# A four-layer gated cross-attention network on one core: plans made in stages, weights, mask, keys and a context moved to other places, biases added by TensorE

## The chip, the cores and the metric

The kernel runs on one core of one Trainium2 chip. A run's time is the device time in microseconds; runs are compared by their medians. Three runs of the kernel before took 1714.19, 1714.95 and 1720.62 us. One further execution was taken by the hardware profiler; its rows are called "the profile" or "the trace" here. Five engines work side by side, each through its own queue of instructions: TensorE (PE for its matmuls, PEld for its weight loads), VectorE (DVE), ScalarE (ACT), GpSimd (POOL) and SyncE (SP), which here only issues DMAs.

## The reference

The input x has 16 sequences of 128 tokens with 256 numbers each, and there is a context of the same shape. Four layers follow each other, each a cross attention and then a feed-forward part; both are added to x after a multiplication by the tanh of a gate:

```
for i in 0..3:
    x = x + tanh(g_xattn[i]) * attention_i(layernorm(x), ctx)
    x = x + tanh(g_ffn[i])   * ffn_i(layernorm(x))
```

Attention 0 has 16 heads and no biases; 1 has biases and takes its softmax over the queries; 2 takes its queries from x and adds a key mask times -1e30, with biases; 3 has 8 heads of 64 and attends over the normed context together with the normed x. Feed-forward 0 routes every token to 2 of 8 experts (GELU, hidden 1024); 1 is a dense layer with a LoRA mixture and a bias; 2 routes to 2 of 8 experts with a clipped SwiGLU and adds a shared expert with a bias; 3 routes to 2 of 8 experts (SiLU, hidden 256). All numbers are float32.

## The kernel before

**Blocks.** Tokens lie on the 128 partitions; x stays in SBUF as 16 tiles of 128x256. Four sequences make a block, so there are four blocks.

**Attention loop.** `attend` (line 1181) writes the order of the instructions of PE, ACT and DVE out by hand: within it these three engines keep program order. A step per sequence emits scores, values of the sequence before and output of the one before that. Between these pieces `tick()` (1193) advances side jobs, which are Python generators: preparing the next block (`prepare`: queries, keys, normed contexts), and the work behind a finished block (`behind`: routing or LoRA). A job yields a number, the count of ticks until its next turn, cut to `most` (5 in layer 0, 99 in layers 1 and 2, 2 in layer 3) and to 1 once the last scores are emitted; from then on a filler, such as expert slots, also takes a turn per tick. Layers 1 and 2 share one call of `attend`. A block's first step waits in the program until its preparing jobs are emitted.

**Work outside that loop**, and DMA issue on SP and POOL inside it, is ordered by a list scheduler with a cost model: it may put an instruction ahead of others that the program creates earlier, where it thinks that an engine is free.

**Routing.** `Moe.front` (360) norms a block, computes router logits, picks two experts for each token with DVE operations of 0.15 to 0.25 us, ranks the tokens with two small matmuls (389) and scatters every token's row twice to DRAM (`xg`) with eight indirect DMAs on POOL (443). `Moe.plan` (497 to 589) then computes, in some 25 DVE operations, which expert each slot of 128 rows has and where its rows begin (`plan_i`, 570); SP reads these numbers into registers. Layer 0 has an early plan after block 1 and a last one after block 3, layer 2 has one, layer 3 three (after blocks 1, 2 and 3). A slot of an early plan needs only the scatters made until then.

**Slots.** `Moe.slots` (591) runs 39 slots of 128 rows per routed layer: SP loads the rows (653) and, where the expert changes, the weights (1256); PE transposes the rows (686), multiplies twice (1303, 1472 or 1520, then 723); POOL scatters the result to `yd` (732). Three lanes of weights take turns. In layer 0 nine early slots run inside the attention loop as its filler, and the others after it.

**What lies where before the change.** The eight DMAs of the attention weights of layers 1 and 2 (815, called at 2043) are created between the early slots and the others of layer 0; `mask_by_keys` (1900), which makes two columns per sequence out of layer 2's mask, right after them. The shared expert's weights (1388) are loaded ahead of the loop of layers 1 and 2. Each layer's keys (1021) are projected one block ahead; only layer 1 makes two blocks of keys at its start. `first_context` (1737) norms layer 3's context of block 0 at the end of layer 2's slots, `context` (1743) the others in the loop. Output biases of attentions 1 and 2, LoRA and the shared expert are scaled with the gate by DVE (281) and added to x by POOL (`add_bias`, 284), 64 operations of 128x256.

**Range check.** The fast path leaves out the softmax maximum. `Watch.see` (972) clamps each reciprocal to a range and adds up what the clamp changed, in three POOL operations; at the end, a count decides whether the whole network is computed again in the general way. It isn't here.

Of the kernel before, what the change touches and what calls it, by code (L numbers as in the profile page):

```python
# [37 lines left out]
TINY, HUGE = 1e-30, 1e30  # L38
# [51 lines left out]
def kernel(ctx: ExitStack, tc: tile.TileContext, a: dict, out: bass.AP):  # L90
# [51 lines left out]
    for e in range(2):  # L142
        nc.gpsimd.memset(ones2[:, e, e, :], 1.0)
# [3 lines left out]
    tg = const.tile([P, 8], F32, tag="tg", name="tg")  # L147
# [11 lines left out]
    nc.gpsimd.memset(nothing, 0.0)  # L159
    region = const.tile([P, NE], F32, tag="region", name="region")  # L160
# [12 lines left out]
    token_i = const.tile([P, B], I32, tag="token_i", name="token_i")  # L173
# [9 lines left out]
    def tgx(i):  # L183
        return tg[:, i:i + 1]

# [15 lines left out]
    def inverse_sd(var, n, twice):  # L201
# [16 lines left out]
        t2 = stat.tile([P, n], F32, tag="nt2", name="nt2")  # L218
        nc.vector.tensor_tensor(t2, t, r0, ALU.mult)
        rstd = stat.tile([P, n], F32, tag="rstd", name="rstd", bufs=4)  # L220
        nc.vector.scalar_tensor_tensor(rstd, t2, 1.5, r0, ALU.add, ALU.mult)
# [38 lines left out]
    def ln_block(blk):  # L260


        mv, rstd = yield from ln_stats([xs[b] for b in block(blk)])
        xns = yield from normalized([xs[b] for b in block(blk)], mv, rstd)
# [14 lines left out]
    def gated_bias(bias_row, gate):  # L279
        gb = rpool.tile([P, D], F32, tag="gbias", name="gbias", bufs=3)  # L280
        nc.vector.tensor_scalar(gb, bias_row, gate, None, ALU.mult)
        return gb

    def add_bias(blk, gb):

        for b in block(blk):
            nc.gpsimd.tensor_tensor(xs[b], xs[b], gb, ALU.add)  # L287

# [57 lines left out]
    class Moe:  # L346
# [4 lines left out]
        def __init__(self, layer, wg, turn):  # L351
            self.layer, self.wg, self.turn = layer, wg, turn
# [7 lines left out]
        def front(self, blk, plan=None):  # L360

            xns, xnT = yield from ln_block(blk)
# [38 lines left out]
            if self.layer == 3:  # L401
                for _ in range(2):
# [44 lines left out]
            if plan is not None:  # L447
                plan()
# [48 lines left out]
        def plan(self, turns, early=False, kind=""):  # L497
# [12 lines left out]
            full = t([P, NE, B], "full")  # L510
# [17 lines left out]
            else:  # L528
                nc.vector.tensor_scalar(skip, cnt, -1.0, float(B), ALU.mult, ALU.add)
            part = t([P, NE, NE], "part")  # L530
# [9 lines left out]
            )  # L540
            eid = t([P, n], "eid")
# [5 lines left out]
            nc.vector.tensor_reduce(ahead, past, AX.X, ALU.add)  # L547
            plan = t([P, 4, n], "plan")
# [9 lines left out]
            nc.vector.tensor_scalar(plan[:, 1], at, float(P), None, ALU.mult)  # L558

# [12 lines left out]
            nc.vector.tensor_scalar(code, plan[:, 0], -1.0, float(NE), ALU.mult, ALU.add)  # L572
            if early:
# [389 lines left out]

    class Watch:


        def __init__(self, n, tag):
            self.off = const.tile([P, n], F32, tag=f"off{tag}", name="off_range")
            nc.gpsimd.memset(self.off, 0.0)
            self.n = n  # L970

        def see(self, r):
            z = stat.tile([P, self.n], F32, tag="wz", name="wz", bufs=1)
            nc.gpsimd.tensor_scalar(z, r, TINY, HUGE, ALU.max, ALU.min)  # L974
            nc.gpsimd.tensor_tensor(z, z, r, ALU.subtract)
            nc.gpsimd.tensor_tensor(self.off, self.off, z, ALU.add)

        def fine(self, good):

            eq = stat.tile([P, self.n], F32, tag="wz", name="wz", bufs=1)  # L980
            nc.vector.tensor_scalar(eq, self.off, 0.0, None, ALU.is_equal)
            nc.vector.tensor_reduce(good, eq, AX.X, ALU.add)
            return self.n * P

    class Fast16:
# [3 lines left out]
        def __init__(self, layer, pool, kpool, w, ctxT, watch, mask=None):  # L989
# [20 lines left out]
        def prepare(self, blk, before):  # L1010
# [5 lines left out]
            if self.layer == 1 and blk == 0:  # L1016

                made.append(self.keys(1))
            return made

        def keys(self, blk):
            layer = self.layer
            wk = self.w[1]
            self.kT[blk] = kT = self.kpool.tile([P, KC, TB], F32, tag="kT", name="kT", bufs=2)
# [11 lines left out]
        def queries(self, blk, before):  # L1036
# [7 lines left out]
            if layer and blk == 0:  # L1044
                self.gb = gated_bias(row(f"l{layer}_bo"), tgx(layer))
            _, xnT = yield from ln_block(blk)
            if layer:
# [1206 lines left out]
```

## Time and profile before

| what | value |
|---|---|
| median of 3 runs | 1714.95 us (1714.19 to 1720.62) |
| the profiled execution's own time | 1761.32 us |
| its span, first to last instruction | 1759.6 us |
| instructions | 34942 |
| PE matmul busy | 1579.3 us (90%) |
| PE weight load busy | 1211.5 us (69%) |
| DVE busy | 897.9 us (51%) |
| ACT busy | 634.4 us (36%) |
| POOL busy | 421.2 us (24%) |
| mean granted TensorE clock | 0.948 |

By the trace the stages are: attention 0 to about 145 us, the nine early slots to 246, the other slots of layer 0 to 447, attentions 1 and 2 with LoRA to 795, the shared expert to 950, slots of layer 2 to 1266, attention 3 to 1568, slots of layer 3 to 1726, the last additions and stores to 1759.6.

Rows of the profile read as follows: the time, then engine, line, operation, written tile "<-" read tiles, shape, count. A bracket tells how long the engine sat idle before the row and which instruction ended that; "issue" means that the profile shows no releaser. Matmuls of float32 appear as two instructions each. A granted clock of 1.00 is TensorE's full speed.

### The profile page before, as it was taken

The numbers are of one execution on the slowest core, as the hardware profiler recorded it, in microseconds if no ns is written. First come the engines' busy times: TensorE is split into PE (matmuls) and PEld (weight loads), VectorE is DVE, ScalarE is ACT, GpSimd is POOL, SyncE is SP. The second block draws the span as 40 slices with busy tenths as digits, with TensorE's granted clock in tenths as the row PEclk, the third lists the DMA queues.
The fourth block names the chain that finished last, engine by engine and source line by source line (L and its number), as shares of the span: only waits on it lengthen the run. The fifth ranks groups of instructions, "written<-read, shape, count | busy, mean of one in ns | idle before, by whom it ended". The sixth has DMA issues, their size and how long they took to land. (4 is left out here: it accounts for less than half of the span.)

```text
span 1759.6 us, 34942 instructions
## 1 busy us (share of the span) xinstructions
PE 1579.3 (90%) x12739; PEld 1211.5 (69%) x12739; DVE 897.9 (51%) x2889; ACT 634.4 (36%) x1502; POOL 421.2 (24%) x546
## 2 busy tenths in 40 slices
PE   7986889999788899899999999999989999896892
PEld 4665779999445566565459999999845655576792
DVE  3665412122476755655555555556553553556454
ACT  5534433345354455434224333334423423122010
POOL 3443311111222223441120110101101112223333
PEclk9988899999889999989999999999999998998896
DMA  9405483443300000000045323401320100033755
GB/s 346 190 26 175 152 290 125 136 137 122 107 25 1 1 1 1 26 25 25 25 147 187 120 76 111 135 29 32 99 67 10 38 4 22 27 100 110 246 160 189
DMA packets 109911, 169.27 MB, mean 96 GB/s; under 512 B 16665, under 2 KB 83678, under 8 KB 109728
## 3 DMA queue, kind: packets, MB, share of 16 engines
q1 hardware_dynamic: 91776, 118.28, 21.2%
q0 software_dynamic: 13392, 43.37, 6.5%
q10 hardware_dynamic: 4560, 5.25, 0.9%
q8 instruction: 107, 1.75, 0.4%
q14 instruction: 76, 0.62, 0.1%
HBM read 268.42 MB, written 48.18 MB: 180 GB/s over the span
## 5 line engine op out<-in xcount | busy, mean ns | idle before, releaser
L1472 PE MATMUL ps_w<-xT,w 128*128 128x128 f32 x2304 | 266.6, 275 | 0.0
L1472 PEld LDWEIGHTS ps_w<-xT,w 128*128 128x128 f32 x2304 | 264.2, 192 | 2.2 <-issue 0.2
L732 POOL DMA_INDIRECT yd<-y,to x117 | 117.7, 1006 | 603.1 <-DVE y L731 379.5
L723 PE MATMUL ps_e<-w,hT 128*128 128x256 f32 x848 | 202.2, 385 | 2.8 <-DVE hT L1386 1.2
L723 PEld LDWEIGHTS ps_e<-w,hT 128*128 128x128 f32 x848 | 157.6, 194 | 23.7 <-PE ps_w L642 2.5
L974 POOL TENSOR_SCALAR wz<-rs 128x256 f32<-128x256 f32 (+1 forms) x64 | 57.9, 904 | 437.5 <-DVE rs L1870 158.3
L1480 ACT ACTIVATE u<-ps_w,b 128x128 f32<-128x128 f32 x312 | 89.5, 367 | 173.9 <-PE ps_w L1472 165.3
L1303 PE MATMUL ps_h<-xT,w 128*128 128x128 f32 x1120 | 136.0, 280 | 8.7 <-DMA w<-in_l_w_dram 4.9
L1483 DVE SCALAR_TENSOR_TENSOR m<-ps_w,b,u 128x128 f32<-128x128 f32 x312 | 87.6, 344 | 105.3 <-PE ps_w L1472 96.0
L1303 PEld LDWEIGHTS ps_h<-xT,w 128*128 128x128 f32 x1120 | 132.2, 197 | 11.2 <-issue 5.8
L731 DVE SCALAR_TENSOR_TENSOR y<-ps_e,c,bias 128x256 f32<-128x256 f32 x78 | 37.6, 483 | 190.6 <-PE ps_e L723 189.7
L1308 ACT ACTIVATE hT<-ps_h,b 128x128 f32<-128x128 f32 x312 | 88.7, 373 | 127.4 <-issue 83.0
L443 POOL DMA_INDIRECT xg<-xn,xi x96 | 93.8, 977 | 100.2 <-issue 86.9
L1408 PE MATMUL ps_w<-xnT,sw 128*128 128x512 f32 x256 | 113.5, 601 | 0.5 <-issue 0.5
L1093 PE MATMUL ps_s<-qM,kT 32*128 32x256 f32 x768 | 79.9, 442 | 14.9 <-ACT e L1108 6.6
L1408 PEld LDWEIGHTS ps_w<-xnT,sw 128*128 128x128 f32 x256 | 48.9, 192 | 59.2 <-issue 53.9
L1159 DVE RECIPROCAL rs<-ps_o 128x256 f32<-128x256 f32 x32 | 56.2, 1756 | 51.1 <-PE ps_o L1148 39.9
L1093 PEld LDWEIGHTS ps_s<-qM,kT 32*128 32x128 f32 x768 | 41.9, 193 | 53.8 <-issue 27.6
L287 POOL TENSOR_TENSOR x<-x,gbias 128x256 f32<-128x256 f32 x64 | 46.2, 747 | 134.4 <-ACT xn L250 69.0
L250 ACT ACTIVATE xn<-x,nmr,rstd 128x256 f32<-128x256 f32 x128 | 67.6, 599 | 21.8 <-DVE nmr L246 20.3
L1148 PE MATMUL ps_o<-e,v 128*32 128x128 f32 x1536 | 61.8, 295 | 11.9 <-issue 7.0
L1108 ACT ACTIVATE e<-ps_s 128x512 f32<-128x512 f32 x128 | 65.8, 600 | 14.8 <-PE ps_s L1093 11.6
(263 smaller groups left out, 2686.2 us busy)
## 6 DMA issues: line engine op xcount, KB each, us to landing
w<-in_l_w_dram SPq DMA_DIRECT2D x156, 1024.0 KB
w<-in_l_w_dram SPq DMA_DIRECT2D x39, 512.0 KB
kT<-in_l_wgu_dram SPq DMA_DIRECT2D x39, 512.0 KB
xg<-zeros POOLq DMA_DIRECT2D x15, 1170.0 KB
yr<-yd SPq DMA_DIRECT2D x40, 256.0 KB
xr<-xg SPq DMA_DIRECT2D x78, 130.0 KB
b<-in_l_b_dram SPq DMA_DIRECT2D x78, 128.0 KB
kT<-in_l_w_dram SPq DMA_DIRECT2D x39, 256.0 KB
```

Of the source, the lines that this page charges most:

```text
L250: nc.scalar.activation(xns[:, i, 0:D], src, AF.Identity, bias=nmr[:, i:i + 1], scale=rstd[:, i:i + 1])
L443: self.unordered(nc.gpsimd.indirect_dma_start(out=xg[:, :], in_=xns[:, i, :], in_offset=None, out_offset=bass.IndirectOffsetOnAxis(ap=xi[: ...
L723: nc.tensor.matmul(po, lhsT=hT[:, f, :], rhs=lane(s)["w2"][:, f, :], start=(f == 0), stop=(f == nf - 1),)
L732: self.unordered(nc.gpsimd.indirect_dma_start(out=yd[:, :], in_=y, in_offset=None, out_offset=bass.IndirectOffsetOnAxis(ap=to[:, 0:1], axi ...
L1093: nc.tensor.matmul(pss[j][:, 2 * c:2 * c + 2, :], lhsT=self.kT[blk][part, c, tok], rhs=self.qM[blk][part, c, :, tok], start=True, stop=True,)
L1108: nc.scalar.activation(e, pss[j], AF.Exp)
L1303: nc.tensor.matmul(ps[:, i, :], lhsT=w["w1"][:, k, f * P:(f + 1) * P], rhs=xT[:, k, :], start=(k == 0), stop=(k == KC - 1),)
L1308: nc.scalar.activation(hT[:, f, :], ps[:, i, :], AF.Gelu, bias=w["b1"][:, f:f + 1])
L1408: nc.tensor.matmul(ps, lhsT=wt[:, k, s, f * P:(f + 1) * P], rhs=xnT[:, k, :], start=(k == 0), stop=(k == KC - 1),)
L1472: nc.tensor.matmul(ps[:, f, :], lhsT=wt[:, k, s, f * P:(f + 1) * P], rhs=xT[:, k, :], start=(k == 0), stop=(k == KC - 1),)
L1480: nc.scalar.activation(u[:, f, :], pair[0][:, f, :], AF.Identity, bias=w["b1"][:, i:i + 1])
L1483: nc.vector.scalar_tensor_tensor(m1[:, f, :], pair[1][:, f, :], w["b3"][:, i:i + 1], u[:, f, :], ALU.add, ALU.mult,)
```

## The change

1. `Moe.plan` becomes a generator that yields five times between its DVE operations, `front` yields once ahead of it, and in layer 3 once more within its weights. So other jobs get turns between the pieces.
2. The mask's DMA is created at the start (`load_mask`); its few operations run as part of the job that prepares block 2 of layer 0.
3. The attention weights of layers 1 and 2 are created at turn 24 of the job of layer 0's later slots (a slot takes three turns) instead of before its first; at the same turn the shared expert's output bias is loaded as a row, and at turn 48 DVE splits four biases into three bfloat16 parts each (`split_biases`, `thirds`).
4. Layer 2's keys of blocks 0, 1 and 2 are made with layer 1's first preparation, those of block 3 with layer 1's block 1. They take the places of the shared expert's weights, which are now loaded ahead of layer 2's last block.
5. Layer 3's second context is loaded and normed at the end of layer 2's slots, and its keys are made at the start of attention 3.
6. The four biases are added by a matmul: `pick` (96x128 bfloat16, three rows of ones) times the three parts, accumulated into the same PSUM tile. `add_bias` and the gated biases go, on the fast path.
7. The range check adds up the values themselves, one POOL operation a step instead of three. The sums of attentions 0, 2 and 3 are made with 2^-12 instead of 1, and the gate takes that factor back. A third watch follows layer 3's norms. Some constants share memory.

The core of the diff:

```diff
@@ Moe.front
             nc.vector.tensor_reduce(cw, sel, AX.X, ALU.add)
             if self.layer == 3:
+                yield 1
...
             if plan is not None:
-                plan()
+                yield 1
+                yield from plan()
@@ Moe.plan (five times, after skip, past, ahead, plan[:, 1] and code)
+            yield 1
@@ Watch
         def see(self, r):
-            z = stat.tile([P, self.n], F32, tag="wz", name="wz", bufs=1)
-            nc.gpsimd.tensor_scalar(z, r, TINY, HUGE, ALU.max, ALU.min)
-            nc.gpsimd.tensor_tensor(z, z, r, ALU.subtract)
-            nc.gpsimd.tensor_tensor(self.off, self.off, z, ALU.add)
+            nc.gpsimd.tensor_tensor(self.sum, self.sum, r, ALU.add)
@@ new: biases on PE
+    def thirds(tag, bias_row, rest):
+        t = rpool.tile([P, D], BF16, tag=tag, name="bias3", bufs=1)
+        first, second, third = (slice(i * 32, (i + 1) * 32) for i in range(3))
+        nc.vector.tensor_copy(t[0:96], bias_row[0:96])
+        nc.vector.tensor_tensor(rest[0:96], bias_row[0:96], t[0:96], ALU.subtract)
+        nc.vector.tensor_copy(t[second], rest[second])
+        nc.vector.tensor_copy(t[third], rest[third])
+        nc.vector.tensor_tensor(rest[third], rest[third], t[third], ALU.subtract)
+        nc.vector.tensor_copy(t[third], rest[third])
+        return t
+
+    def add_row(ps, t):
+        nc.tensor.matmul(ps, lhsT=pick[0:96, :], rhs=t[0:96, :], start=False, stop=True)
@@ Fast16.output (the same in Lora.run and shared2)
-                    start=(k == 0), stop=(k == KC - 1),
-                )
-            add_scaled(b, py, tgx(self.layer))
+                    start=(k == 0), stop=(k == KC - 1 and self.bias is None),
+                )
+            if self.bias is not None:
+                add_row(py, self.bias)
+            add_scaled(b, py, self.gate)
@@ Fast16.prepare
-            if self.layer == 1 and blk == 0:
-                made.append(self.keys(1))
+            if self.others is not None:
+                if blk == 0:
+                    made.append(self.keys(1))
+                for later in (0, 1, 2) if blk == 0 else (3,) if blk == 1 else ():
+                    made.append(self.others.keys(later))
@@ Fast16.queries
-            if layer and blk == 0:
-                self.gb = gated_bias(row(f"l{layer}_bo"), tgx(layer))
             _, xnT = yield from ln_block(blk)
-            if layer:
-                add_bias(blk, self.gb)
@@ Fast3
-        def first_context(self):
-            self.first = t = self.wpool.tile([P, KC, TB], F32, tag="first", name="kv_first")
-            cmv, crs = finish(ln_stats(self.cts))
-            finish(self.turned(t, self.cts, cmv, crs, "media_w", "media_b", True))
+        def first_contexts(self):
+            self.normed = {}
+            for blk in range(2):
+                if blk == 0:
+                    t = self.wpool.tile([P, KC, TB], F32, tag="first", name="kv_first")
+                else:
+                    t = xtpool.tile([P, KC, TB], F32, tag="xnT", name="kvc")
+                    self.cts = self.load_context(blk)
+                cmv, crs = finish(ln_stats(self.cts))
+                finish(self.turned(t, self.cts, cmv, crs, "media_w", "media_b", True))
+                self.normed[blk] = t
...
         def prepare(self, blk, before):
-            return [self.residual(blk, before), self.context(blk)]
+            made = [self.residual(blk, before)]
+            if blk != 1:
+                made.append(self.context(blk))
+            if blk == 0:
+                made.append(self.context(1))
+            return made
@@ layers
+                mi = load_mask(cpool)
...
+                    if blk == 2 and fast:
+                        mask.extend(mask_by_keys(cpool, mi))
...
-            ws = [attention_weights(layer, wpool) for layer in (1, 2)]
-            if fast:
-                mask = mask_by_keys(wpool)
...
-                finish(slots0(moe, NSLOT - n, plans[-1:], lanes, tiles(fpool, bufs0)))
+                job = slots0(moe, NSLOT - n, plans[-1:], lanes, tiles(fpool, bufs0))
+                for i, _ in enumerate(job):
+                    if i == 24:
+                        ws = [attention_weights(layer, wpool) for layer in (1, 2)]
+                        if not biases:
+                            t = stat.tile([P, BPB, ROW], F32, tag="xn", name="bias_rows", bufs=3)
+                            nc.sync.dma_start(
+                                out=t[:, 0, 0:D],
+                                in_=a["l2_b2"][NE:NE + 1].to_broadcast([P, D]),
+                            )
+                    if i == 48 and not biases:
+                        split_biases(t)
...
+            def load_shared(blk):
+                if blk == NBLK - 1:
+                    sw.extend(shared_weights(spool))
+                yield 1
...
-                for n, _ in enumerate(slots2(moe2, plans, pool, get)):
-                    if n % (2 * BPB) == BPB and n // (2 * BPB) < NBLK:
-                        add_bias(n // (2 * BPB), gb)
+                finish(slots2(moe2, plans, pool, get))
                 if fast:
-                    att.first_context()
+                    att.first_contexts()
```

## The prediction

> **What bounds the kernel now.** I read the page first: matmuls fill 90% of the span, no other engine passes 51%. So added matmul time costs, and a gain must come from TensorE's idle time. Next I asked for busy time by stage. Columns: stretch in us, its length, busy time of PE, PEld, DVE, ACT and POOL with instruction counts, granted clock, DMA share, GB/s.
>
> ```profile
> 162.00:250.00 88.00, 73.13 (x446) 65.93 (x445) 29.60 (x153) 33.13 (x87) 25.25 (x26) 0.90 0.56 184
> 446.00:475.00 29.00, 20.11 (x76) 10.04 (x75) 12.55 (x37) 9.91 (x18) 6.67 (x11) 0.82 0.31 86
> 475.00:640.00 165.00, 144.50 (x1230) 88.90 (x1222) 117.58 (x322) 76.56 (x155) 39.66 (x83) 0.94 0.04 12
> 640.00:795.00 155.00, 141.05 (x1521) 92.00 (x1518) 89.45 (x234) 71.90 (x125) 61.71 (x73) 0.94 0.04 15
> 950.00:1266.00 316.00, 314.93 (x2547) 304.64 (x2546) 186.37 (x635) 125.02 (x380) 39.01 (x37) 1.00 0.28 92
> 1266.00:1291.00 25.00, 18.09 (x56) 9.14 (x55) 11.93 (x32) 8.04 (x15) 2.16 (x2) 0.92 0.29 94
> 1568.00:1640.00 72.00, 46.25 (x355) 41.41 (x346) 45.96 (x243) 15.53 (x26) 25.89 (x27) 0.87 0.35 117
> ```
>
> The expert slots of layer 2 (950 to 1266) are full. The idle time lies at seams: 15 us in 162 to 250, 9 at 446, 7 at 1266, 26 in 1568 to 1640. The timeline, read across each, says who is late (start, duration, engine, line; in brackets the idle time before and its releaser):
>
> ```profile
> 169.20 0.17 DVE L1907 CAST mask_f<-mask_i 128x16 f32<-128x16 int32 x1 [5.34 <-DMA mask_i<-in_mask_dram]
> 170.28 0.61 PE L389 MATMUL ps_rank<-both,tri 128*128 128x32 f32 x2 [5.17 <-DVE both L384]
> 171.59 5.03 PE L723 MATMUL ps_e<-w,hT 128*128 128x256 f32 x16
> 180.25 3.62 PE L723 MATMUL ps_e<-w,hT 128*128 128x256 f32 x16
> ...
> 248.58 0.41 PE L686 MATMUL ps_xr<-ident,xr 128*128 128x128 f32 x2 [1.73 <-DMA xr<-xg]
> 251.49 6.13 PE L1303 MATMUL ps_h<-xT,w 128*128 128x128 f32 x32 [2.50 <-DMA w<-in_l_w_dram]
> ...
> 446.92 7.03 PE L828 MATMUL ps_k<-ctxT,w_att 128*128 128x512 f32 x16
> 461.95 2.16 PE L271 MATMUL ps_ln<-ident,xn 128*128 128x128 f32 x8 [8.00 <-ACT xn L250]
> 464.79 5.27 PE L828 MATMUL ps_q<-xnT,w_att 128*128 128x512 f32 x8 [0.68 <-ACT xnT L275]
> ...
> 1589.63 2.04 PE L1520 MATMUL ps_g<-xT,kT 128*128 128x128 f32 x8 [7.04 <-issue]
> ```
>
> The mask's cast waits for its DMA in DVE's queue, between two steps of routing block 2, although the program creates it later. At 1589 "issue" hides a wait too: xT of that slot is copied at 1589.12, after a DVE chain of routing and plan since 1579.26.
>
> [...] the same 16 matmuls took 5.03 us after the 5.17 us stall and 3.62 us later. A stall removed thus returns more than its length. [...]
>
> **The change part by part** (likeliest; both ends).
>
> *Mask early*: -6.6 (5.2 idle, 5.03-3.62=1.4 slow clock). The next thing due is the second weight of slot 2, issued at 176.66, so I take -6 (-7; -2). The mask's DMA moves onto POOL's queue near the start, before the zero fills from 12.64 us; it holds POOL 1.27 us and nothing on DVE waits before block 2. Cover: POOL sat idle 6.64 us before the zeros.
>
> *Plans in stages, layer 0, blocks 0-1*: PE idles 6.42 us at 132 to 138.57, since ACT's logarithm waits behind DVE's plan (131.38 to 135.13), and the exponentials behind it. Splitting removes that. But the first slot's rows wait for eight scatters on POOL (132.26 to 142.2), are asked for at 144.41, and its weight, behind them on SP, at 145.73; it lands before 150.92, where PE already waits 2.39. None of this moves, so PE arrives earlier and waits: 0 (-3; +3).
>
> *Second plan of layer 0*: a 2.29 us gap at 219.97, behind plan operations from 214.33 to 218.9: -2 (-2.3; 0). It now takes five more turns of the filler, three per slot of about 7.3 us: 12 us, ready near 226, before SP wants it at 237.
>
> *Weights within slots*: SP issues eight attention weights from 236.77 to 242.2 ahead of the next slot's rows (243.14) and weight (244.43). Without them these start 6 us earlier: 1.73+2.50 and 6.13-3.73=2.4 of slow clock, 6.6. The eight issues (5.4 us of SP) and 2 MB come back within the slots, where PE is busy 193 of 196 us and weights are fetched two slots ahead: cover of about 14 us. I take -5 (-6.6; 0). New beside them: one row by DMA and some 27 DVE operations of 0.2 to 0.35 us that split the biases, about 7 us on a DVE busy 39 of 196. A slot's copy of xT has about 3.6 us of slack (one ps_e): +1 (0; +8, if they wait for the row's DMA as the cast does).
>
> *Keys of layer 2 in layer 1*: one block of keys is 7.03/2=3.5 us. Three go to the seam at 447, one (in place of layer 2's first) into layer 1's block 0; layer 2 loses 10.5 us, of which PE's 141 of 155 busy lets me count 9.5. At the seam keys now end at 446.92+5x3.5=464.4; ACT must clear the last (0.69) before the logarithm behind it, then 0.4, four DVE steps 0.65, first xn 0.65: 466.8 to 467, 5 us later than 461.95. [...] ps_q 3.5 instead of 5.27, -1.7. Sum -9.5+5-1.7=-6 (-9; -2).
>
> *Biases on PE*: 64 matmuls of 256 bf16 columns (16 each in attention 1 and 2, LoRA, shared expert). The trace has no stream of them. [...] a fp32 pass of 256 columns took 3.62/16=226 ns. From above: an isolated one took 272 ns with a weight load of 98 (the rows of "nothing"), 0.37. [...] I take 0.12: 7.7. In attention 1, where PE is idle 20 of 165 us, a little hides: +7 (+4; +20). The 64 POOL additions removed (0.73 each) made one wait of 0.5 us: 0. The range checks fall from three POOL operations to one; POOL is no bound: 0. The other small constants are hidden before PE's first matmul at 8.72.
>
> *Layer 3's second context*: norm and transposes go ahead of the seam at 1266, eight transposes (1.0 us) into ACT's evacuation of the first. Its keys (16 matmuls, 7.1 us) move to the seam, yet do not fill the 3.96 us gap at 1287.91: statistics on DVE stand behind three copies of values that PE produces after all keys, so the gap moves 7 us later whole. Attention 3 loses 8.2, the seam gains 7: -1 (-3; +6, if DVE inside the slots waits for the late context).
>
> *Plans in stages, layer 3*: in 1568 to 1640 PE is busy 46 of 72 us, DVE 46. The large stalls are 7.04 (plan of block 2), 5.97 at 1631.05 and 3.52 at 1639.76 (plan and scatters of block 3), with half clock after each (ps_g 2.04 against 1.13). DVE's total stays; spread over nine turns it lies beside 1.5 us of matmul per turn. From below, only block 3's scatters come earlier: -3. From above, all three stalls and their slow clock: 16.5+5. I take -10 (-20; -2). What is late next: the 22 last slots cannot load before block 3's scatters land (1638); 17 earlier slots of 3 us cover that.
>
> Sum: -6+0-2-5+1-6+7-1-10=-22 us on a profiled 1761.3 (span 1759.6 and 1.7 around it): 1739. The median of the runs shown is 1714.95, 46 below; -22/1761.3=-1.25% of it gives 1694.
>
> **Rivals.** *Given back* (1715; 0.15): biases at their upper end cost 20 instead of 7, and the tail gains 3 instead of 10: -22+13+7=-2. For it: PE is the bound; the first plan's stall already has a DMA wait to fall into. Against: the tail has 26 us idle. *More* (1672; 0.10): the whole tail (-20) and the seams at their ends: -22-10-5-3-2=-42. *Slower* (1731; 0.20): waits that the scheduler places. Work outside the attention loops is reordered, as the mask's cast shows, and the changed text has two new chains with a DMA at their head: the bias row in layer 0's slots, the second context in layer 2's. If a DVE operation is put ahead of its late DMA, each slot behind it stalls. SP's longest wait for a lane in the trace is 14 us; two such waits, each with 5 us of slow clock, give +38: -22+38=+16. It decides from 22+8.6=31 us of new waiting. For it: the 5.34 us precedent. Against: bnst of the first context, hoisted to 948.7, waited for nothing. That the change doesn't take place is excluded for the keys and biases: the order on PE is written out.
>
> **Chances.** Forecast 0.55, more 0.10, given back 0.15, slower 0.20. A difference of 0.5% (8.6 us) is about what a measurement of this kernel can tell from none: faster 0.65, same 0.15, slower 0.20. The forecast's own range is 1680 to 1706; the range of eight in ten cuts half of "more" and the upper third of "slower": 1673 to 1730.
>
> **What would show it.** No DVE wait on the mask near 163; rows of the next slot asked for at about 237 instead of 243; keys to 464 at the first attention seam and a gap under 3 us; at layer 3's seam a gap still near 4; new rows of 64 bf16 matmuls, about 0.12 us of spacing each; the stretch of 72 us at the tail near 62. Wrong if DVE waits for DMAs inside the slots of layers 0 or 2 or if slots2 exceeds its 316 us, if the bias matmuls cost over 0.3 us, or if 1568 to 1640 keeps its length because another wait takes over.

## The result, and the profile after

| | before | after |
|---|---|---|
| median of 20 runs | 1714.57 us (1710.73 to 1720.62) | 1710.95 us (1704.80 to 1716.72) |
| ratio, with its 95% interval | 1 | 0.9973 (0.9961 to 0.9986) |
| profiled execution, its span | 1714.13, 1712.4 us (second profile) | 1708.5, 1706.8 us |

The change gains 3.6 us, a sixth of the 22 forecast, and lies within the 0.5% that was called no change. The forecast's own range was 1680 to 1706 us.

The profile that the prediction was read from took 1761.32 us. The kernel before was therefore profiled once more; the expectation on record said what each outcome would mean:

> The kernel before, unchanged, profiled once more. Its first profile took 1761.32 us, 46 above the median of its timed runs (1714.57), while the profile of the changed kernel (1708.5) lies at its median. Theory A, the first profile shows the kernel's usual stalls, only in a slower execution: this profile again takes 1750 us or more, or it is shorter evenly over all stages. Theory B, the first profile was a single odd execution, with stalls that the timed runs don't have: this one takes 1710 to 1722 us, the layer 0 slots after the early ones (first at 246.5, keys at 446.9 there) take near 180 instead of 200 us and attention 3 (1291 to 1568) near 255 instead of 277, while the tail (1568 to 1640) keeps 72. Then the seam and slot terms of the prediction were read from stalls that usually aren't there.

It took 1714.13 us, and its span of 1712.4 us compares with the 1706.8 after. Most of the stalls that the prediction priced are there again (7.52 instead of 8.00 us at the first seam, 7.04 and 6.13 for the first two of the tail's three), so they weren't odd. The third of the tail, 3.52 us at 1639.76, is not: the 13th slot's first matmul begins 74.8 us after the first slot's rows, against 79.9 in the first profile. The outcome is theory B's in the time and in attention 3 (280.2 us from the transposes of its first context to the first slot's rows, 298.9 in the first profile), not in layer 0's later slots, which take 200 us in both. What the second profile lacks is mainly another kind of stop, treated below with the standing PE. Levels near 1714 and near 1760 us both came back in later runs, so each row of experiments (kernels that were timed together) is read by its ratio to the kernel before in that row.

Busy time by stage, of the second profile of the kernel before. The cuts are the first transposed slot rows of layer 0, the first keys of layer 1, the first slot rows of layer 2, the first keys of layer 3, the first slot rows of layer 3 and its last output matmul. Columns as in the prediction.

```profile
0.00:144.20 144.20, 117.80 (x1497) 80.96 (x1497) 87.31 (x258) 69.47 (x141) 67.79 (x119) 0.93 0.50 183
144.20:434.60 290.40, 273.23 (x1864) 253.79 (x1862) 74.08 (x344) 120.19 (x370) 58.48 (x61) 0.98 0.53 171
434.60:911.20 476.60, 433.91 (x3202) 260.89 (x3201) 291.62 (x796) 199.51 (x359) 135.58 (x198) 0.95 0.11 37
...
1247.80:1525.80 278.00, 265.51 (x2552) 164.10 (x2552) 141.06 (x380) 86.83 (x179) 53.47 (x61) 0.99 0.12 39
1525.80:1679.50 153.70, 129.41 (x942) 115.72 (x936) 92.82 (x421) 26.66 (x55) 53.68 (x56) 0.94 0.53 168
```

The same stages of the changed kernel:

```profile
0.00:147.40 147.40, 113.92 (x1498) 76.78 (x1499) 87.50 (x265) 69.68 (x141) 45.06 (x97) 0.92 0.48 176
147.40:425.50 278.10, 268.49 (x1859) 249.26 (x1860) 80.17 (x362) 119.78 (x370) 54.15 (x55) 0.99 0.53 172
425.50:903.90 478.40, 446.42 (x3265) 268.18 (x3264) 280.86 (x793) 199.57 (x359) 54.02 (x71) 0.95 0.13 42
...
1242.60:1515.60 273.00, 262.98 (x2548) 163.50 (x2546) 138.94 (x367) 84.41 (x173) 27.24 (x34) 0.99 0.13 39
1515.60:1672.70 157.10, 131.35 (x940) 117.01 (x936) 92.50 (x423) 26.50 (x55) 52.28 (x55) 0.93 0.52 165
```

The second number of each row is the stage's length. Attention 0 grew by 3.2 us, the slots of layer 0 lost 12.3, layers 1 and 2 up to the slots grew by 1.8, attention 3 lost 5.0 (2.1 of them came back at the stage left out, 336.6 to 338.7), the tail grew by 3.4. So by stages the gain lies near where it was forecast, in layer 0's slots and attention 3, and both ends of the kernel got longer.

**The first end.** The timelines of DVE, ACT and PE of the changed kernel in its first 27 us (start, duration, engine, line; in brackets the idle time before and its releaser):

```profile
11.95 0.71 DVE L229 SCALAR_TENSOR_TENSOR nt<-r,ve 128x4 f32<-128x4 f32 x1 [1.49 <-ACT r L226]
22.33 0.29 DVE L2003 TENSOR_SCALAR rows<-rows 128x256 f32<-128x256 f32 x1 [9.67 <-DMA rows<-in_rows_dram]
22.54 0.15 DVE L230 TENSOR_TENSOR nt<-nt,r 128x4 f32<-128x4 f32 x1
...
23.28 2.08 ACT L261 ACTIVATE xn<-x,nmr,rstd 128x256 f32<-128x256 f32 x4 [10.06 <-DVE nmr L257]
...
24.02 2.07 PE L284 MATMUL ps_ln<-ident,xn 128*128 128x128 f32 x8 [11.43 <-ACT xn L261]
```

Line 2003 is the first operation of `split_biases`, which the program creates at turn 48 of layer 0's later slots; the part of it that reads a row loaded at turn 24 ran at 308 us. The other rows that it reads are loaded once, at the kernel's start, so nothing ties it to turn 48: the scheduler put it between two steps of the first norm, where it waits 9.67 us for a DMA that SP issued at 10.33. The first norm ends behind it. Before, these transposes began at 13.77, 10.2 us earlier. How much of that reaches the kernel's end is a question of its own: from there to the first slot's rows it is 123.4 us now and was 130.4.

**The other end.** DVE, POOL and PE in the tail of the changed kernel:

```profile
1549.62 0.17 DVE L1017 TENSOR_SCALAR wz<-sum_range 128x4 f32<-128x4 f32 x1 [5.18 <-POOL sum_range L1012]
1588.89 0.15 DVE L745 TENSOR_SCALAR to<-c 128x1 int32<-128x1 f32 x1 [3.97 <-DMA yd<-y,to]
...
1549.35 0.24 POOL L1012 TENSOR_TENSOR sum_range<-sum_range,rstd 128x4 f32<-128x4 f32 x1
...
1535.16 2.05 PE L1573 MATMUL ps_g<-xT,kT 128*128 128x128 f32 x8 [2.77 <-issue]
1542.27 1.13 PE L1573 MATMUL ps_g<-xT,kT 128*128 128x128 f32 x8 [2.57 <-ACT lv L224]
1551.36 2.08 PE L1573 MATMUL ps_g<-xT,kT 128*128 128x128 f32 x8 [3.61 <-DVE xT L724]
1563.39 1.13 PE L1573 MATMUL ps_g<-xT,kT 128*128 128x128 f32 x8 [2.46 <-issue]
1573.13 1.13 PE L1573 MATMUL ps_g<-xT,kT 128*128 128x128 f32 x8 [2.52 <-issue]
1590.44 2.05 PE L1573 MATMUL ps_g<-xT,kT 128*128 128x128 f32 x8 [3.87 <-DVE xT L724]
```

Line 1017 is the final test of the new third range check, 128x4 numbers that were meant for the end of the kernel. Their last input is an addition on POOL, queued behind eight scatters (the last begins at 1547.08). DVE waits 5.18 us for it, and with DVE the copy of xT and PE, 3.61. In the second profile of the kernel before, PE's stops here were these:

```profile
1548.66 2.05 PE L1520 MATMUL ps_g<-xT,kT 128*128 128x128 f32 x8 [7.04 <-issue]
...
1572.50 1.13 PE L1520 MATMUL ps_g<-xT,kT 128*128 128x128 f32 x8 [2.47 <-issue]
...
1578.79 1.13 PE L1520 MATMUL ps_g<-xT,kT 128*128 128x128 f32 x8 [1.89 <-issue]
...
1589.11 1.22 PE L723 MATMUL ps_e<-kT,hT 128*128 128x256 f32 x2 [6.13 <-DVE hT L1527]
```

The stages did cut the 7.04 us stop (2.77+2.57 now) and the 6.13 one (3.87, and that for another reason). But block 3's scatters did not come earlier. Here are the first slot's rows and the first of these scatters, in the changed kernel and, below the dots, in the kernel before with its 13th slot:

```profile
1515.61 0.44 PE L722 MATMUL ps_xr<-ident,qT 128*128 128x128 f32 x2
1573.49 0.99 POOL L473 DMA_INDIRECT xg<-xn,xi  x1 [4.14 <-issue]
...
1525.85 0.44 PE L686 MATMUL ps_xr<-ident,qT 128*128 128x128 f32 x2
1583.77 0.96 POOL L443 DMA_INDIRECT xg<-xn,xi  x1 [0.30 <-issue]
1600.68 1.13 PE L1520 MATMUL ps_g<-xT,kT 128*128 128x128 f32 x8
```

The scatters begin 57.9 us after the first slot's rows in both, and the 13th slot's first matmul (1590.44 and 1600.68) 74.8 us after them in both. The early slots ran faster; then DVE waited 3.97 us for a buffer of row numbers, and PE 3.87. The slots behind take about 3.0 us each in both, except the 13th: after its stop it runs at half clock (0.50 granted from 1589.36 to 1596.18) and takes 5.7 us, against 3.4 before. That is 2.3 of the 3.4 us by which the tail grew.

### The profile page after: what moved, and what is told of

It is laid out like the page before. It is cut to its first block, busy times and chain, and to the rows that moved or that the text cites. A ratio compares the mean times of both kernels' runs of the same rounds, so it can differ in the third digit from the quotient of the medians.

```text
span 1706.8 us, 34879 instructions
## 1 busy us (share of the span) xinstructions
PE 1557.9 (91%) x12803; PEld 1197.2 (70%) x12803; DVE 892.7 (52%) x2915; ACT 636.6 (37%) x1504; POOL 285.2 (17%) x364
## 5 line engine op out<-in xcount | busy, mean ns | idle before, releaser
L759 PE MATMUL ps_e<-w,hT 128*128 128x256 f32 x848 | 197.8, 380 | 3.0 <-DVE hT L1430 1.3
L1012 POOL TENSOR_TENSOR sum_range<-sum_range,rs 128x256 f32<-128x256 f32 x48 | 35.2, 733 | 426.7 <-DVE rs L1203 187.7
L1573 PE MATMUL ps_g<-xT,kT 128*128 128x128 f32 x296 | 44.4, 296 | 24.4 <-DVE xT L724 11.5
L751 ACT ACTIVATE bias<-b,c 128x256 f32<-128x256 f32 x78 | 40.3, 517 | 64.1 <-DMA b<-in_l_b_dram 25.2
```

Source lines behind the costliest of these rows:

```text
L759: nc.tensor.matmul(po, lhsT=hT[:, f, :], rhs=lane(s)["w2"][:, f, :], start=(f == 0), stop=(f == nf - 1),)
```

## The experiments

The theory was: **work of the change that the scheduler put ahead of late inputs ate the gain** (start 10.2 us, range check 5.4 with the slow clock behind it, 0.50 granted from 1551.36 to 1555.2). Its rival: these stops are hidden, and the loss lies in the biases, the keys or the plans. All kernels but the last were run at the 1760 us level; the last at 1713. With intervals of 0.2 to 0.3% to either side, a difference of less than some 6 us between two kernels of a row can't be told from none (an estimate from the intervals in the table).

| kernel | ratio to before in its row | 95% interval |
|---|---|---|
| changed kernel (after_again) | 1.0008 | 0.9988 to 1.0028 |
| split_late | 0.9958 | 0.9941 to 0.9974 |
| watch_dve | 0.9988 | 0.9972 to 1.0004 |
| both (four rows) | 0.9953, 0.9942, 0.9947, 0.9959 | about ±0.002 each |
| both_out | 0.9943 | 0.9921 to 0.9964 |
| bias_pool | 0.9941 | 0.9916 to 0.9965 |
| keys_back | 0.9942 | 0.9922 to 0.9963 |
| weights_first | 0.9976 | 0.9960 to 0.9992 |
| one_context | 0.9950 | 0.9922 to 0.9978 |
| mask_late | 0.9945 | 0.9924 to 0.9966 |
| plans_whole (three rows) | 0.9916, 0.9900, 0.9912 | about ±0.003 each |
| twice (1713 us level) | 1.0053 | 1.0034 to 1.0071 |

**split_late: the split can't go to the start.** Its rows are loaded at turn 24 into the tile that is split.

```diff
+    for j, name in enumerate(("l1_bo", "l2_bo", "base_b")):
+        nc.sync.dma_start(out=t[:, 1 + j, 0:D],
+            in_=a["rows"][:, slice(*_ROWS[name])].to_broadcast([P, D]))
...
-    biases[name] = thirds(name, row(name), t[:, 1 + i, 0:D])
+    biases[name] = thirds(name, t[:, 1 + i, 0:D], t[:, 1 + i, 0:D])
```

> The changed kernel (1710.95 us), but the split of the biases reads rows that are loaded at turn 24 of the layer 0 slots, so the scheduler can't put it at the kernel's start. Theory H (work put ahead of its late DMA eats the gain): the 9.67 us wait of DVE on the rows at 22.33 us goes, the first transposes of the norm start near 14 us instead of 24.02, and nothing later takes it back: 10.2 us less, near 1701. Rival R (the stall is hidden by later waits, for scatters and weights, and the gain was lost elsewhere, to the biases on PE or the keys): less than 3 us less, 1708 or more.

**watch_dve: the third check adds on DVE**, `nc.vector` for `nc.gpsimd` in its `see`.

> The changed kernel, but the third range check's four numbers a block are added up by DVE instead of POOL. Theory H: the final test of that sum, put into DVE's queue at 1549.62 us, no longer waits 5.18 us for POOL's scatters; PE's 3.61 us stop at 1551.36 and the slow clock behind it (2.08+1.91 us for 16+16 matmul instructions that take 1.13+1.06 at full clock, so 1.8) go: 5.4 us less, near 1705.5. Rival R: PE meets the next wait (plan and scatters of the same block) and less than 1.5 us is gained, 1709.5 or more.

**both: the two edits together.**

> Both edits. Theory H: they lie 1500 us apart and add up, 15.6 us less than the changed kernel, near 1695, 1.1% below the kernel before, which is where the prediction had its change. Rival R: 1705 or more.

**both_out**, as both, and 14 buffers for the row numbers.

```diff
-    return rpool.tile(shape, dtype, tag=tag, name=tag, bufs=OUT)
+    return rpool.tile(shape, dtype, tag=tag, name=tag, bufs=OUT if tag == "c" else OUT + 6)
```

> Both edits, and 14 instead of 8 buffers for the slots' row numbers (to) in layer 3. In the changed kernel DVE waits 3.97 us at 1588.89 for such a buffer, since the returns that read them stand behind block 3's eight scatters on POOL, and PE stops 3.87 us at 1590.44. Theory H: the wait goes, with the slow clock behind it (1.8) 5.7 us less than with both edits alone, near 1689.5. Rival R: the eight buffers of y wait for the same returns instead, and the time stays within 1.5 us of both edits alone.

In this row the kernel before takes 1761.8 us, and the changed kernel was not in it; the next row has it.

> The changed kernel itself, so that the others of this row have it on their own chip: the row before ran where the kernel before takes 1761.8 us, and the changed kernel wasn't among it. Theory H (hoisted work eats the gain) on a chip where the kernel before takes about 1714: 0.9973 of it again; where it takes about 1761: 0.998 to 1.000, since split_late stood at 0.9958 there and the start costs 9 to 10 us (0.55%). Rival R (the edits in split_late and both gained nothing): as split_late, 0.996.

> Both edits again, beside the changed kernel. Theory H: 0.9 to 1.0% below the changed kernel where the kernel before takes 1714 us (10.2 at the start and 5.4 at the third range check: 1695); where it takes 1761, PE paused by itself at the very place of the range check (DVE idle 6.02 us behind PE), so only the start's 10 us are left: 0.55% below it. Rival R: within 0.2% of it.

At this level the changed kernel is no faster than the kernel before (1.0008), and both edits are 0.66% faster than it in the same row, 11.6 us, against 10 expected there; their intervals don't meet. In split_late's own profile the first transposes begin at 14.5 us. In the two profiles of this row nothing takes the late start back: from the first transposes to the first slot's rows it is 133.0 us in both (23.3 to 156.3 and 14.5 to 147.5). So at this level the start's stop is real and nothing hides it. The range check can't be told: watch_dve and the changed kernel overlap, and both equals split_late within the row (0.9953, 0.9958). At the 1713 us level one trace shows both stops gone: in the last kernel below, which has both edits, the fifth slot begins 5.3 us after the fourth instead of 9.1, the first transposes at 14.65. But that kernel, which also has eight more scatters per block on POOL, reaches the first slot's rows only 4.1 us before the changed kernel (143.3 and 147.4) and layer 1's keys 2.1 us after it (427.6 and 425.5). So what the two edits gain at the level of the result was not measured, and it is open how much of the start's 10.2 us is hidden there.

both_out shows nothing (0.9943 beside 0.9953), and at this level it couldn't: neither in its profile nor in that of both does DVE wait for such a buffer. PE stops 9.2 us at block 3's scatters in both, for the reason treated below.

**bias_pool: biases on POOL as before**, no split, no bias matmul (`add_bias` and the gated biases back in their places, `add_row` out).

> Both edits, but the four biases are added by POOL as before the change, so no split and no bias matmul. As predicted (7 us for 64 matmuls of about 0.12 us): 7 us less than both_again. Rival (a bias matmul costs the upper 0.3 us, and more with the wait in front of the copy): 20 us less. Second rival (PE waits in the attentions anyway, and the 64 POOL additions stood in the way of something): no change or 3 us more.

No change that the row can tell: the second rival. The trace has what the term was built from, rows of the bias matmul:

```profile
L316 PE MATMUL ps_y<-bias,pick 96*128 96x256 bf16 x32 | 8.9, 279 | 0.0
```

Each is followed by the next matmul after 114 ns in the median (0.12 taken, an estimate of mine that no trace had shown), so 64 of them fill 7.3 us of PE. The kernel doesn't get longer by it; whether PE would have waited anyway, or the 64 POOL additions cost as much, is not settled.

**keys_back, weights_first, one_context, mask_late** each undo one move in the kernel with both edits: `later` keys taken out and the shared weights back at the loop's start; `ws = [...]` ahead of the slots; `range(1)` contexts; the mask loaded and made behind attention 0.

> As both_third, but layer 2's keys are made in layer 2 again and the shared expert's weights come at the start of the loop. As predicted (-6): 6 us more than both_third. Rival (three blocks of keys at the first seam only move the seam, 14.6 to 19.8 us, and layer 2 was waiting anyway): within 2 us.

> As both_third, but the eight attention weights are asked for before the later slots of layer 0. As predicted (-5): 5 us more than both_third. Rival (the eight issues cost the same within the slots): within 2 us.

> As both_fourth, but only the first context of layer 3 is normed ahead. As predicted (-1): 1 us more, not to be told from none. Rival (its late DMA stalls DVE in layer 2's slots, or its keys only fill the seam): 3 us less.

> As both_fourth, but the mask is loaded and made after attention 0 as before the change. As predicted (-6): 6 us more. Rival (the new place costs a stop of its own: 1.70 us of PE at 55.75 and 1.4 us of slow clock behind it in the changed kernel's profile): 3 us more.

Only the weights' move shows at all: without it the kernel takes 0.29% more than both_third, 5.1 us for 5 forecast, with intervals that just overlap (by the medians, 2.2 us). Its profile agrees: layer 0's slots take 293.3 us, against 284.1 to 287.2 in the four profiles with both edits. Keys, second context and mask are not told from nothing (forecast 6, 1 and 6). In mask_late's profile the cast holds DVE again, 6.2 us, and PE 4.2; the time doesn't show it.

**plans_whole: plans in one piece**, in the kernel with both edits. The five yields within the plan stay in the text under a condition that is never true; the one ahead of the plan and the one within layer 3's weights are out.

```diff
 @@ Moe.plan, five times
-            yield 1
+            if self.layer < 0:
+                yield 1
 @@ Moe.front
             if self.layer == 3:
-                yield 1
...
             if plan is not None:
-                yield 1
                 yield from plan()
```

> Both edits, but plans are computed in one piece again in all layers. As predicted (2 us in layer 0, 10 in the tail of layer 3): 12 us more than both_again. Rival (by the trace of the changed kernel the tail's stalls only moved: 20.6 us before, 18.2 after without the range check's; attention 0 gained 3.4 of its 6.43 us stall): 3 to 6 us more.

> Both edits (bias split late, third range check on DVE) a third time, as the reference of this row. Where the kernel before takes about 1714: 0.989 of it if hoisted work alone ate the gain (10.2 us at the start, 5.4 at the range check, from 0.9973); 0.992 if only the start counts. Where it takes about 1760: 0.994 to 0.995 again.

> As both_third, with plans in one piece. Theory T (the tail's length is the chain norm, router, ranking, eight scatters of block 3 and then the last 26 slots of 3 us, which a plan in stages doesn't shorten: slot 13 starts 74.8 us after the first in both profiles): within 3 us of both_third, or below it. The prediction's term (stages gain 12 us in all): 12 us above both_third.

> Both edits, as the reference of this row. Where the kernel before takes about 1714 us: 0.988 to 0.989 of it (0.9973 less 10.2 us at the start and 5.2 at the third range check). Where it takes about 1760: 0.994 to 0.995, as three times before.

> As both_fourth, with plans in one piece. Theory P (on the one chip PE stands still while POOL issues eight scatters, unless it is waiting for a plan anyway; on the other it doesn't): where the kernel before takes about 1760, 6 to 8 us less than both_fourth, as twice before; where it takes about 1714, 3 to 6 us more than both_fourth, since the stages then save the 3.4 us of attention 0 and some 2 us of the tail that the trace shows. Rival (stages cost by themselves, through later plans): less than both_fourth on either chip.

Three rows agree: plans in one piece take 0.26, 0.47 and 0.47% less than the same kernel with plans in stages, about 7 us, where 12 us more had been forecast. In each row alone the two intervals overlap or touch; it is the three together that tell. This is the fastest kernel of the study, 0.84 to 1.00% below the kernel before at the 1760 us level. In the profiles the tail takes 161.4 to 166.8 us with stages (four) and 156.8 to 160.1 without (three); attention 0 up to the first slot 2 to 5 us more with stages.

**Why stages cost there.** The kernel with both edits in its tail, PE, DVE, ACT and POOL:

```profile
1576.10 1.06 PE L1576 MATMUL ps_u<-xT,kT 128*128 128x128 f32 x8
...
1578.70 1.91 PE L284 MATMUL ps_ln<-ident,xn 128*128 128x128 f32 x8 [0.46 <-issue]
1585.26 2.07 PE L1576 MATMUL ps_g<-xT,kT 128*128 128x128 f32 x8 [4.65 <-DVE xT L724]
...
1625.69 2.05 PE L1576 MATMUL ps_g<-xT,kT 128*128 128x128 f32 x8 [9.18 <-issue]
...
1583.81 0.42 DVE L1583 TENSOR_TENSOR hT<-ps_u,sg 128x256 f32<-128x256 f32 x1 [6.02 <-remote]
...
1583.90 1.07 ACT L288 COPY xnT<-ps_ln 128x512 f32<-128x512 f32 x2 [3.78 <-remote]
...
1577.20 0.97 POOL L473 DMA_INDIRECT xg<-xn,xi  x1 [0.30 <-issue]
1578.47 0.97 POOL L473 DMA_INDIRECT xg<-xn,xi  x1 [0.30 <-issue]
```

The rows say that PE had done ps_u by 1577.2 and the transposes by 1580.6. DVE and ACT, which wait for just these, go on at 1583.8, both at once: PE's semaphore (the counter by which it tells the others that it is done) is silent from 1573.8 on, then counts five updates within 0.3 us. "remote" means that no row's end lies near the release.

Counted over all traces, with 3 us as the limit for how far the semaphore may come behind PE's rows, each of the 17 profiles at the 1760 us level has 7 to 12 such stretches, and all but four of the 145 end within about 13 us of the first of a block's eight scatters on POOL. The three profiles at the 1713 us level (the second of the kernel before, the changed kernel's, the last kernel's below) have none. The record has holes as well: in those 17 profiles 45 to 59 of PE's some 1550 updates are missing, in these three none. So how late an update came is only roughly known; that DVE and ACT stood idle until 1583.8 doesn't hang on it.

With plans in one piece PE is idle through such a stretch anyway, waiting for DVE's plan; with stages it has slots in hand and is held: 7.0 to 7.5 us in four profiles of this block, 0 to 1.6 in three with plans in one piece. At block 3's scatters PE stops 6.2 to 9.2 us in the four and 5.1 to 5.4 in the three. That this is how stages lose their 7 us is argued from these traces; no run tests it.

**twice: is it the scatters?** As both, and behind each block's scatters eight more of the same rows into a tensor that nothing reads.

```diff
+            for i in range(BPB):
+                for j in range(2):
+                    self.unordered(nc.gpsimd.indirect_dma_start(
+                        out=xg2[:, :], in_=xns[:, i, :], in_offset=None,
+                        out_offset=bass.IndirectOffsetOnAxis(ap=xi[:, j, i:i + 1], axis=0),
+                    ).ins, self.extra, "extra")
```

> Both edits, and behind each block's eight scatters eight more of the same rows into a second DRAM tensor that nothing reads. Where the kernel before takes about 1760 us: in the profiles so far PE's semaphores stand still only while POOL issues a block's scatters (in the kernel with both edits 9.7 us in the third block, 7.4 in the eleventh). Theory S (the scatters hold PE up): the stops last until the sixteenth scatter, some 8 to 10 us longer in the blocks where PE has work, and the kernel takes 30 to 70 us more than both edits alone. Rival C (the stops only happen to lie there, from PE's own code): they keep their length and place, and the time rises by no more than 10 us, through the returns that queue behind them on POOL. Where the kernel before takes about 1714 us: no stops in either, and 0 to 10 us more.

In this row the kernel before takes 1713 us; PE doesn't stand still there, and sixteen scatters don't make it. So scatters alone aren't the cause; at the 1760 us level cause or coincidence stays open, and so does what makes the levels. The result files name the same chip number for a row of each, so it is not shown to be the chip. The time (1.0053) is not 0 to 10 us above both edits as expected there, if those are near 0.99; but both edits alone weren't run at this level. So either the extra scatters cost more than 10 us or the edits gain less here than expected. One reading is firm. In the tail:

```profile
1604.26 0.15 DVE L752 TENSOR_SCALAR to<-c 128x1 int32<-128x1 f32 x1 [11.42 <-DMA yd<-y,to]
...
1605.78 2.05 PE L1583 MATMUL ps_g<-xT,kT 128*128 128x128 f32 x8 [10.91 <-DVE xT L731]
```

Eight more scatters, 10.2 us of POOL, turn the wait for a row number's buffer from 3.97 into 11.42 us and PE's stop from 3.87 into 10.91. So that last stop of the changed kernel hangs on POOL's queue: the returns that free the buffers stand behind block 3's scatters. It took the place of the plan's stop. The same trace shows what the range check did to the stages: here, without its wait, block 3's scatters begin 54.5 us after the first slot's rows (1580.26 and 1525.81), 3.4 us earlier than the 57.9 of the changed kernel and of the kernel before.

## Why the prediction was wrong, step by step

22 us were forecast and 3.6 measured. Two steps failed by their mechanism: where the split and the range check would run, and what the stages of layer 3's plans would return. Several smaller terms can't be told from nothing. The time is the one that the rival "given back" named, but not for its reason: it let the biases cost 20 us, and bias_pool shows no such cost. The right figure there is luck.

*Biases split in layer 0's slots* (+1, 0 to +8). The place was wrong: its first operation ran at 22 us and put the first norm 10.2 us later. At the 1760 us level this and the range check cost 11.6 us together; at the level of the result their cost is open. I had read the mask's cast, put ahead of its DMA, as the warning it was, and built the "slower" rival on it, but looked for such waits where the program creates the work: the bias row in layer 0's slots, the context in layer 2's. Neither waited. What waited had inputs that seemed ready from the start. The two waits of DVE are 9.67+5.18=14.9 us, under the 31 that I gave as the point from which that rival decides, and the kernel did stay a little faster. The 5 us of slow clock that this rival put behind each wait were an estimate of mine: ahead of the last stores, the first profile has 0.50 granted for at most 10.24 us at a stretch (457.75 to 467.99, for one), half of which is 5.1.

*Range check* (0). "POOL is no bound" was the wrong question. The third check adds a test on DVE whose input comes over POOL's queue: 5.18 us of DVE, 3.61 of PE.

*Plans in stages, layer 3* (-10, -20 to -2): measured +3.4 at the level of the result, with the range check's stop in it, and at the other level a loss of about 7 us for all plans. The step that failed is the sum of three stalls as if each could be had alone. One of them, 3.52 us, isn't in the second profile. The two others got shorter, but the next wait took the time: the returns that free the buffers stand on POOL behind block 3's scatters, and these begin at the same 57.9 us. I had written the rule myself for the first plan of layer 0: what PE saves, it waits at the next gate. "17 earlier slots of 3 us cover that" held before the change too; time saved in these slots moves no scatter. The lower end, "only block 3's scatters come earlier: -3", fits the last kernel's 3.4 us; in the changed kernel it was 0.

*Attention 0* (0, -3 to +3): 7.0 us shorter after the late start. 3.4 of it is the first plan's stop, 6.43 to 3.06, in spite of the gate named. PE's own busy time also fell, from 114.1 to 110.2 us for the same matmuls, at a mean granted clock of 0.94 instead of 0.92. The last kernel, with the split put late, has 113.8 us at 0.92, so part of this may belong to the late start and not to the stages.

*Layer 0's slots* (-6-2-5+1=-12): -12.3. The sum is right; of its parts the runs support only the weights (5.1 us by weights_first). As forecast no DVE operation waits for the mask near 163, and PE's stop there, 4.15 us in the second profile, is gone. But at 55.75 PE stops 1.70 us for the cast, in attention 0's fixed order, and mask_late is not told from both edits: I priced the moved DMA's queue and left out the two matmuls that moved with it. They explain a part of the 6 us; where the rest went is open. The second plan's stop (2.29 us, priced at 2) is 3.07 us in the second profile and 2.27 in the changed kernel, and both times the DMA of a weight ends it: the plan was not what PE waited for.

*Keys* (-6) *and biases on PE* (+7): +1 together, +1.8 measured to the slots of layer 2, each nothing by its own run. The seam is as drawn, keys to 442.8 and a gap of 2.53 us:

```profile
425.48 17.33 PE L864 MATMUL ps_k<-ctxT,w_att 128*128 128x512 f32 x40
445.33 2.17 PE L284 MATMUL ps_ln<-ident,xn 128*128 128x128 f32 x8 [2.53 <-ACT xn L261]
448.17 5.94 PE L864 MATMUL ps_q<-xnT,w_att 128*128 128x512 f32 x8 [0.68 <-ACT xnT L288]
```

but ps_q took 5.94 us, not 3.5. That it would run at full clock behind so short a gap was an estimate of mine that no trace had shown. After this stop of 2.53 us the granted clock went from 1.00 to 0.50 at 445.89, 0.6 us into the transposes, and stayed there to 452.72. The length alone doesn't decide it: after stops of 2.57, 2.46 and 2.52 us in the tail of the same profile (shown above) the granted clock was 1.00 and ps_g ran in 1.13 us.

*Second context* (-1): the 3.96 us gap at layer 3's seam stayed to the hundredth, as forecast, and the move is worth nothing.

*The median.* I scaled the sum by -1.25% from a profile 46 us above the median. Most of the stalls used are in the faster profile too (not the 3.52 us one), so this isn't the main error. But its idle time holds stops that the rule of "what waits for what" doesn't explain, and a second profile was the way to see it.

## What to carry to other kernels

Where a list scheduler orders the work, ask of each new operation not where the program creates it, but how early its inputs let it go, and what stands behind it then: two small operations that nobody needed yet held DVE for 14.9 us here. Tie such work to data that come late. And before stalls on one chain are added up, find the gate that sets the chain's end; a stall ahead of it is worth nothing alone.

## What the runs showed of the hardware that was not expected

At the 1760 us level PE's semaphore stands still for up to 9.7 us, nearly always about the time in which POOL issues a block's eight scatters (10 us), in all of 17 profiles; at the 1714 us level not once in three, not even with sixteen scatters. The cause is open. Half clock (0.50 granted) followed one stop of 2.53 us, and full clock (1.00) followed stops of 2.46 to 2.57 us in the same profile. An indirect DMA takes 0.97 us of POOL and 0.30 us to the next, and eight more of them turned a wait of 3.97 us for a buffer into 11.42. A bf16 matmul of 96 rows and 256 columns behind float32 ones took its successor 114 ns later.
